# A two-layer graph attention kernel: VectorE's order woven, softmax totals behind the attends, and a new end

## The chip, the cores and the metric

The kernel runs on one core of a Trainium2 chip. The metric is device time in microseconds (us), the median of several runs. Its engines have short names in the profile: PE (TensorE, matmuls; PEld is its weight load), DVE (VectorE), ACT (ScalarE), POOL (GpSimd) and SP (SyncE, which here issues nearly all DMAs).

## The reference, cut to what matters

64 graphs of 256 nodes have 512 features each, and a dense 0/1 adjacency. Two layers follow one another, all in float32:

```python
# layer 0
feat_proj = feats @ fc_w.T + fc_b
logits = q + k.T                               # q, k: one column each, from feat_proj
masked = logits + (1.0 - adj) * -1e9
atten = softmax(where(masked >= 0, masked, 0.01 * masked))
x1 = atten @ feat_proj + feats
# layer 1, 8 heads of 64
Q, K, V = x1 @ W_q + b_q, x1 @ W_k + b_k, x1 @ W_v + b_v
scores = Q @ K.T / 8 + a[:, None] + c[None, :] + b_g + log(adj + 1e-9)   # a, c = x1 @ halves of w_g
out = softmax(scores) @ V + x1
```

## The kernel before

The 64 graphs make 32 groups of two (512 tokens). The kernel is one software pipeline: a step of it works at the same time on up to four groups, named D (done but for its last division and store), A (layer 1's attention), F (layer 0's weighted sum and all projections) and X (the next group: its loads and layer 0's weights). There is no scheduler: `step` and `attention_and_layer_0` write the order out by hand as strings of pieces, such as `A("both:0 parts:0 turn_residual:1")`. Each piece issues instructions to several engines, and every engine runs what it has been given in exactly that order. So a piece's place in the strings sets its place in each engine's queue, and in SP's queue of DMAs too.

The projections are products of 512 x 512 matrices by Strassen's scheme with seven block products, here called `p1` to `p7` (class `Product`, matmuls in L404). For each of `pf` (layer 0's features), `pq`, `pk` and `pv`: VectorE first makes four sums of the moving blocks (`ysum:0..3` for pf, `xsum:0..3` for the others, L344 and L369); the products accumulate in PSUM; ScalarE copies what is kept (`keep`), and VectorE adds the quarters (`sum_00`, `sum_11`, `sum_10`, L432; for pf L490, with GpSimd adding x to the kept part in L484). `p4` accumulates on the bank that `sum_11` has to read first.

x1 must also be had transposed. Each quarter of x1 is turned in 32 x 32 blocks by VectorE (`send`, L781), written to DRAM (xd, L785) and read back in four pieces (`fetch`, L793) into `x1T`. `keys:t` (L508, jc) are dot products of x1's rows with half of w_g. `dot_q:t` and `dot_k:t` are those of the next group's x with the rows of layer 0 (L508, jq and jk), and `spread` sends the q dots through DRAM to all partitions (qrow).

Layer 1's attention: `scores:u` (L850, exponentials in L859) for four units u (graph and half of the heads), `factor:u:jc` multiplies the exponentials by the adjacency (L867). The softmax denominators go by `both:u` (adds two tiles, es, L875) and `parts:u` (turns the sum in blocks, est, L905, then reduces it, L906); `totals:gr` sums over partitions by a matmul with a matrix of ones (L915), and `ratios:gr` takes reciprocals (L927). `attend:gr` is the product with V (L888, copied to oTs in L895). Then `turn:gr` (osb, L967), `divide:gr` (L987), `complete:gr` (adds the residual xb, L995), `store:gr` (L1028). `residual:gr` and `turn_residual:gr` make xb out of x1T (xv, L818 and L832). For layer 0, `add_tiles`, `parts_0` and `recip` do what both, parts and totals do.

Most tiles that matter have one buffer per tag: `x`, `adj`, `oTs`, `es`, `e0`, `osb`. A load into x waits until the last reader of the older x is done, and so for adj.

The last step (no next group) has an order of its own. Behind it a check that all reciprocals were in range (`in_range`) sets a flag, and a branch on the flag skips a general version of the kernel.

## Time and profile before

| | |
|---|---|
| median of 3 runs | 2330.38 us (2330.05 to 2332.13) |
| the profiled execution | 2331.22 us |
| its span, first to last instruction | 2329.4 us |
| granted TensorE clock, mean | 0.998 |
| PE, DVE, ACT, POOL busy | 2293.2, 2202.7, 1080.2, 125.5 us |
| DMA | 163.84 MB |

Busy is the time in which an engine had an instruction under way. Matmuls overlap each other in the records: a matmul of 256 columns is shown with some 380 ns, and the next starts 216 ns after it. So of PE a length of a stretch says more than a sum of durations.

### The profile page before, as it was taken

To read this page: it belongs to the slowest core of one execution; us is meant where nothing else is said; L and a number is where in the kernel's file an instruction comes from. 1 tells how busy PE (TensorE), PEld (TensorE's weight loads), DVE (VectorE), ACT (ScalarE), POOL (GpSimd) and SP (SyncE) were. 2 spreads that over 40 slices of the span, in tenths; PEclk is the share of its full clock that TensorE was granted. 3 is DMA by queue.
4 is the path that set the end of the run, shared out by engine and by line. 5 is a ranking of instruction groups with operands and counts; after the bars stand their busy time and mean duration, and the time that the engine had idled before them with its cause. 6 is when DMAs were issued, how large, how long until landed. Compare 5 with 4: busy or idle time off the path is not lost.

```text
span 2329.4 us, 33749 instructions
## 1 busy us (share of the span) xinstructions
PE 2293.2 (98%) x12554; PEld 1902.1 (82%) x12554; DVE 2202.7 (95%) x3212; ACT 1080.2 (46%) x2121; POOL 125.5 (5%) x120
## 2 busy tenths in 40 slices
PE   9999999999999999999999999999999999999996
PEld 5888888888888888888887888888888888888885
DVE  6799999999999999999999999999999999999996
ACT  3554345453445544455534455444554344554443
POOL 0000000000000000000000000000000000000000
PEclk9999999999999999999999999999999999999999
DMA  4123323222322232232233222332222333223312
GB/s 131 41 64 73 78 73 69 59 69 77 87 73 57 64 75 77 73 68 60 69 81 82 73 51 60 85 78 73 63 63 70 78 80 75 56 61 84 78 46 38
DMA packets 517265, 163.84 MB, mean 70 GB/s; under 512 B 415188, under 2 KB 478696, under 8 KB 517096
## 3 DMA queue, kind: packets, MB, share of 16 engines
q1 hardware_dynamic: 514440, 160.32, 29.0%
q8 instruction: 101, 1.65, 0.3%
q10 hardware_dynamic: 2656, 1.31, 0.2%
q14 instruction: 68, 0.56, 0.1%
HBM read 95.43 MB, written 66.12 MB: 69 GB/s over the span
## 4 chain that ended last, share of the span: by engine, by line
PE 56%; DVE 31%; DMA 5%; issue 4%; SPq 2%; ACT 1%; DVEq 0%; POOL 0%; ACTq 0%; POOLq 0%
PE pk L404 11%; PE pq L404 10%; PE pf L404 9%; PE pv L404 9%; PE y L678 6%; PE sc L850 5%; DVE e L867 5%; PE oT L888 5%; DVE est L905 2%; DVE es L875 2%; DVE x L490 2%; DMA xd<-xt 2%; DVE jc L508 2%; DVE tb L344 2%; DVE e L593 1%
## 5 line engine op out<-in xcount | busy, mean ns | idle before, releaser
L859 ACT ACTIVATE e<-sc,c 128x512 f32<-128x512 f32 x512 | 299.6, 736 | 68.6 <-PE sc L850 68.6
L867 DVE TENSOR_TENSOR e<-e,am 128x1024 f32<-128x1024 f32 x256 | 293.4, 1219 | 0.0
L484 POOL TENSOR_TENSOR pf_s<-pf_s,x 128x512 f32<-128x512 f32 x93 | 121.9, 1311 | 2118.2 <-ACT pf_s L483 2049.5
L850 PE MATMUL sc<-qT,kT 64*128 64x256 f32 x2048 | 230.7, 380 | 0.0
L678 PE MATMUL y<-e,x 128*128 128x256 f32 x992 | 228.8, 384 | 0.0
L888 PE MATMUL oT<-e,v 128*64 128x256 f32 x2048 | 228.3, 381 | 0.0
L850 PEld LDWEIGHTS sc<-qT,kT 64*128 64x128 f32 x2048 | 196.4, 187 | 32.1 <-issue 10.6
L678 PEld LDWEIGHTS y<-e,x 128*128 128x128 f32 x992 | 183.6, 190 | 32.7 <-ACT e L859 10.3
L888 PEld LDWEIGHTS oT<-e,v 128*64 128x64 f32 x2048 | 144.2, 137 | 80.2 <-issue 11.0
L895 ACT COPY oTs<-oT 128x512 f32<-128x512 f32 x128 | 72.0, 588 | 260.9 <-DVE osb L967 132.3
L421 ACT ACTIVATE pq_s<-pq,cols 128x256 f32<-128x256 f32 x192 | 80.6, 471 | 233.9 <-DVE qT L432 141.5
L905 DVE STREAM_TRANSPOSE est<-es 128x1024 f32<-128x1024 f32 x124 | 153.1, 1235 | 3.2
L906 DVE TENSOR_REDUCE part<-est 128x32 f32<-128x1024 f32 x124 | 151.3, 1220 | 4.2
L875 DVE TENSOR_TENSOR es<-e,e 128x1024 f32<-128x1024 f32 x126 | 153.3, 1217 | 0.4
L483 ACT ACTIVATE pf_s<-pf,recip 128x256 f32<-128x256 f32 x186 | 77.5, 467 | 156.4 <-PE pf L404 156.4
L418 ACT COPY pk_s<-pk 128x512 f32<-128x512 f32 x96 | 56.3, 586 | 170.0 <-PE pk L404 137.2
L404 PE MATMUL pq<-x1T,wq 128*128 128x256 f32 x512 | 122.8, 383 | 4.5 <-DMA x1T<-xd 3.9
L404 PE MATMUL pv<-wv,t1b_c 128*128 128x256 f32 x512 | 122.7, 382 | 0.0
L404 PE MATMUL pk<-t1b,wk 128*128 128x256 f32 x512 | 121.1, 379 | 0.5 <-DVE kT L432 0.5
L404 PE MATMUL pq<-t1b,wq 128*128 128x256 f32 x512 | 121.4, 380 | 0.0
L404 PE MATMUL pv<-wv,t1b 128*128 128x256 f32 x512 | 121.1, 379 | 0.0
L404 PE MATMUL pk<-t1b,k_s 128*128 128x256 f32 x512 | 120.9, 379 | 0.0
(175 smaller groups left out, 4514.5 us busy)
## 6 DMA issues: line engine op xcount, KB each, us to landing
x<-in_x_dram SPq DMA_DIRECT2D x32, 1024.0 KB, 5.3
xd<-xt SPq DMA_DIRECT2D x124, 256.0 KB, 2.0
x1T<-xd SPq DMA_DIRECT2D x496, 64.0 KB, 2.0
out_dram<-xb SPq DMA_DIRECT2D x248, 128.0 KB, 3.1
adj<-in_adj_dram SPq DMA_DIRECT2D x128, 128.0 KB, 3.6
qrow<-q SPq DMA_DIRECT2D x31, 256.0 KB, 4.1
fc_nat<-in_L_gnn_fc_w_dram ACTq DMA_DIRECT2D x4, 256.0 KB, 4.8
wq<-in_L_gnn_W_q_dram SPq DMA_DIRECT2D x1, 1024.0 KB
```

What stands on the lines that cost most here:

```text
L404: nc.tensor.matmul(o, lhsT=lk[:, ts(m, P)] if len(lk.shape) == 2 else lk[:, m], rhs=rk, start=(start and m == 0 and k == 0), stop=(m == 1 ...
L421: nc.scalar.activation(dst[:, m], src[:, m], AF.Identity, bias=self.bias[:, 2 * o + m : 2 * o + m + 1],)
L483: nc.scalar.mul(s[:, m], src[:, m], self.recip[:, TPG * k + m : TPG * k + m + 1])
L484: nc.gpsimd.tensor_tensor(s, s, self.out(o, k), ALU.add)
L678: nc.tensor.matmul(y[:, ts(gr, N)], lhsT=self.x[:, gr * TPG + j, ts(c, P)], rhs=self.e0[:, j, gr, :], start=(gr == 0 and j == 0), stop=(gr ...
L850: nc.tensor.matmul(sc[par][:, pr, :], lhsT=self.kT[rows, 2 * hg + pr, ts(t, P)], rhs=self.qT[rows, 2 * hg + pr, ts(gr, N)], start=True, st ...
L859: nc.scalar.activation(e[:, par], sc[par], AF.Exp, bias=self.c[:, t : t + 1], scale=SCALE)
L867: nc.vector.tensor_tensor(ef, ef, self.am[:, jc, u // 2, :].unsqueeze(1).to_broadcast([P, 4, N]), ALU.mult,)
L875: nc.vector.tensor_tensor(self.esum[u], self.e[u, 0], self.e[u, 1], ALU.add)
L888: nc.tensor.matmul(oT[par * HD : (par + 1) * HD, pr, :], lhsT=self.v[:, gr * TPG + jc, ts(h, HD)], rhs=self.e[2 * gr + hg, jc][:, par, pr, :],
L905: nc.vector.transpose(turned, self.esum[u].rearrange("p a b i -> p (a b i)"))
L906: nc.vector.tensor_reduce(self.part[:, hg, :], turned.rearrange("p (m c) -> p m c", c=B), AX.X, ALU.add,)
```

## The change

The weights of layer 0 are cut into two pieces (`logits`, `leaky`), `parts` into `est` and `part_of`, `parts_0` into `turn_0` and `part_0`, and the pieces of one chain are placed apart, with pieces of other chains in between. `both`, `est` and `part_of` of the first two units go ahead of `attend:0`; `totals:0` becomes `totals_0`, behind the attends, with two matmuls of half the width, and `ratios_0` takes one reciprocal. `residual:1` writes its xv into the buffer of adj instead of that of oTs, and `turn_residual:1` goes behind the attends. `load_adj` goes from the top of a step to a place just ahead of `load_x`. The range check is made every 3 groups instead of every 4 or so (six slots of reciprocals instead of four). In the last step, the scores come in another order and ahead of most of pv, both graphs' sums are matmuls over the exponentials (`sums_of_e`), `finish` is cut in halves, and the check runs ahead of the last attend.

```diff
-    NR = 4
+    NR, NCHECK = 6, 3
...
                 def residual(self, gr):
-                    self.xv = one.tile([P, NC, N], F32, tag="oTs", name=f"xv_{self.g}_{gr}")
+                    tag = ("oTs", "adj")[gr]
+                    self.xv = one.tile([P, NC, N], F32, tag=tag, name=f"xv_{self.g}_{gr}")
...
+                def totals_0(self):
+                    half = NC * N // B // 2
+                    self.tot = bank(f"tot_{self.g}_0")[:, 0 : 2 * half]
+                    for par in range(2):
+                        nc.tensor.matmul(
+                            self.tot[par * HD : (par + 1) * HD, :].rearrange("p (a m) -> p a m", a=2),
+                            lhsT=every[:, 0:HD], rhs=self.part[:, :, par * half : (par + 1) * half],
+                            start=True, stop=True, skip_group_check=True,
+                        )
+
+                def ratios_0(self):
+                    self.rs = recip1[:, (self.g + 1) % NR, 0]
+                    nc.vector.reciprocal(self.rs.rearrange("p m b -> p (m b)"), self.tot)
...
             def attention_and_layer_0(D, A, F, X):
                 A("scores:0 scores:1 scores:2 scores:3")
-                F("add_tiles parts_0")
-                A("factor:0:0 factor:0:1 factor:1:0 factor:1:1")
-                A("factor:2:0 factor:2:1 factor:3:0 factor:3:1")
+                F("add_tiles")
+                A("factor:0:0")
+                F("turn_0")
+                A("factor:0:1")
+                F("part_0")
+                A("factor:1:0 factor:1:1 factor:2:0 factor:2:1 factor:3:0 factor:3:1")
                 F("mix:0 mix:1 recip mix:2 mix:3 ysum:0")
-                D("ratios:1 divide:1")
-                A("residual:1")
-                F("ysum:1")
+                D("ratios:1")
+                D("divide:1")
+                A("both:0 residual:1")
+                F("ysum:1 ysum:2")
+                A("est:0 part_of:0")
                 D("complete:1 store:1")
-                F("ysum:2 pf.p1 pf.keep_1 pf.p2 pf.p6 pf.sum_00 begin send:0:0 fetch:0:0 ysum:3")
-                A("both:0 parts:0 turn_residual:1")
-                F("pf.p7 pf.p5 pf.p3 pf.add_01 pf.sum_11 send:1:1")
-                A("attend:0")
-                F("pf.sum_01 send:0:1 fetch:1:1 fetch:0:1")
-                A("both:1 turn:0 attend:1 parts:1")
-                F("copy:0 pf.p4 pf.sum_10 send:1:0 fetch:1:0")
-                F("pq.p1 pq.keep_1 pk.p1")
-                A("totals:0")
-                F("pk.keep_1 pv.p1 pv.keep_1")
+                F("pf.p1 pf.keep_1 pf.p2 pf.p6 pf.sum_00 begin send:0:0 fetch:0:0 ysum:3")
+                A("both:1 est:1")
+                F("pf.p7 pf.p5 pf.p3 pf.add_01 pf.sum_11")
+                A("part_of:1")
+                F("pf.sum_01 send:1:1 send:0:1 fetch:1:1 fetch:0:1")
+                A("attend:0 turn:0 attend:1 totals_0 turn_residual:1")
+                F("copy:0 keys:2 pf.p4 pf.sum_10 keys:3 send:1:0 fetch:1:0")
+                F("pq.p1 pq.keep_1 pk.p1 pk.keep_1 pv.p1 pv.keep_1")
...
-                X("load_adj")
...
-                F("xsum:0 xsum:1 xsum:2 pq.p6")
-                F("keys:2 keys:3 keys:0 keys:1")
-                X("load_x")
-                A("ratios:0 both:2 parts:2")
+                F("xsum:0 keys:0 xsum:1 keys:1")
+                X("load_adj load_x")
+                F("xsum:2 pq.p6")
+                A("both:2 ratios_0 est:2 divide:0 part_of:2")
                 F("pq.p7 pq.p2 pq.sum_00 xsum:3")
-                check()
+                X("dot_q:0")
+                A("complete:0 store:0")
+                X("dot_q:1")
                 F("pq.p5 pk.p6 pq.sum_11 pq.p3")
-                A("divide:0")
-                X("dot_q:0 dot_q:1 dot_q:2 dot_q:3 spread")
+                X("dot_q:2")
+                A("turn:1")
+                X("dot_q:3 spread")
                 F("pq.p4 pq.sum_10 copy:1 copy:2")
-                A("complete:0 store:0 turn:1")
+                X("adjt dot_k:0")
+                A("both:3")
+                X("dot_k:1")
+                F("pk.p7 pk.p5 pk.sum_11 residual:0")
+                X("dot_k:2")
+                F("pk.p2 pk.sum_00")
+                X("dot_k:3")
+                F("turn_residual:0")
+                A("est:3")
+                F("pk.p3 pk.p4 pk.sum_10")
                 if n is None:
-                    A("both:3 parts:3")
-                F("pk.p7 pk.p5 pk.sum_11 residual:0")
-                X("adjt")
-                F("pk.p2 pk.sum_00")
-                X("dot_k:0 dot_k:1")
-                F("pk.p3 pk.p4 pk.sum_10")
-                X("dot_k:2 dot_k:3")
-                F("turn_residual:0")
-                if n is None:
-                    A("totals:1 ratios:1 divide:1 complete:1 store:1")
-                    F("residual:1 turn_residual:1")
-                    F("pv.p2 pv.p6 pv.sum_00 scores:0 scores:1 scores:2 scores:3")
-                    F("pv.p7 factor:0:0 factor:0:1 factor:1:0 factor:1:1 both:0 both:1")
-                    F("pv.p5 pv.sum_11 pv.p3 sums_1:0 pv.p4 pv.sum_10")
-                    F("factor:2:0 factor:2:1 ratios_t:0 ratios_r:0 factor:3:0 factor:3:1")
-                    F("attend:0 finish:0 sums_of_e:1 attend:1")
-                    F("ratios_t:1 ratios_r:1 finish:1")
-                    check_ranges()()
+                    A("part_of:3 totals:1 ratios:1")
+                    F("residual:1 pv.p6 scores:2 scores:3 scores:0 scores:1")
+                    A("divide:1 complete:1 store:1")
+                    F("factor:2:0 factor:2:1 factor:3:0 factor:3:1 pv.p7 pv.p5 pv.p3")
+                    F("factor:0:0 factor:0:1 pv.sum_11 turn_residual:1 factor:1:0 factor:1:1")
+                    F("sums_of_e:1 sums_of_e:0 attend:1 ratios_t:1 ratios_r:1 ratios_t:0 ratios_r:0")
+                    F("pv.p2")
+                    flag_ready = check_ranges()
+                    F("finish:1:0 pv.sum_00 pv.p4 finish:1:1 pv.sum_10 attend:0")
+                    flag_ready()
+                    F("finish:0:0 finish:0:1")
                     return
                 X("mask add_eps")
                 F("pv.p6 pv.p7")
-                X("weights:0")
-                F("pv.p5 pv.p2")
-                X("weights:1")
-                F("pv.sum_11 pv.p3 pv.p4 pv.sum_00")
-                A("both:3 parts:3")
+                X("logits:0:0 logits:0:1")
+                A("part_of:3")
+                X("logits:1:0 leaky:0 logits:1:1")
+                F("pv.p5 pv.p2 pv.sum_11")
+                X("leaky:1")
+                F("pv.p3 pv.p4 pv.sum_00")
+                check()
                 F("pv.sum_10")
```

More of the change, by code (lines that the diff above doesn't have):

```diff
@@ L226, in rows_of_chunks @@
                 return t
-            rows_0 = rows_of_chunks([q_w[0], k_w[0], fc_b], "rows_0", "sms")
+            rows_0 = rows_of_chunks([q_w[0], k_w[0], fc_b], "rows_0", "oTs")
             x_0 = load_x(0)
-            rows_1 = rows_of_chunks([b_q, b_v], "rows_1", "sms1")
+            rows_1 = rows_of_chunks([b_q, b_v], "rows_1", "es")
             qb = row(q_b, "qb")
@@ L587, in weights, with logits, leaky @@
                 def weights(self, jc):
-                    e = self.e0[:, jc].rearrange("p g i -> p (g i)")
-                    for gr in range(GP):
-                        t = gr * TPG + jc
-                        eg = self.e0[:, jc, gr].rearrange("p (t n) -> p t n", t=TPG)
-                        nc.vector.scalar_tensor_tensor(
-                            eg, self.qrow[:, :, ts(gr, TPG)].rearrange("p n t -> p t n"),
-                            self.kq[:, 0, t : t + 1], eg, ALU.add, ALU.add,
-                        )
+                    for gr in range(GP):
+                        self.logits(jc, gr)
+                    self.leaky(jc)
+                def logits(self, jc, gr):
+                    t = gr * TPG + jc
+                    eg = self.e0[:, jc, gr].rearrange("p (t n) -> p t n", t=TPG)
+                    nc.vector.scalar_tensor_tensor(
+                        eg, self.qrow[:, :, ts(gr, TPG)].rearrange("p n t -> p t n"),
+                        self.kq[:, 0, t : t + 1], eg, ALU.add, ALU.add,
+                    )
+                def leaky(self, jc):
+                    e = self.e0[:, jc].rearrange("p g i -> p (g i)")
                     nc.vector.scalar_tensor_tensor(e, e, 0.01, e, ALU.mult, ALU.max)
@@ L604, in add_tiles, with turn_0 @@
                     nc.vector.tensor_tensor(es0, e0[:, 0], e0[:, 1], ALU.add)
-                def parts_0(self):
-                    turned = two.tile([P, TOK], F32, tag="xt", name=f"es0t_{self.g}")
+                def turn_0(self):
+                    self.es0t = two.tile([P, TOK], F32, tag="xt", name=f"es0t_{self.g}")
                     if self.older is None:
@@ L615, in parts_0, with part_0 @@
                         self.parts_all = self.older.part_all
-                    nc.vector.transpose(turned, self.es0)
+                    nc.vector.transpose(self.es0t, self.es0)
+                def part_0(self):
                     nc.vector.tensor_reduce(
-                        self.parts_all[:, ALL - TOK // B : ALL], turned.rearrange("p (m c) -> p m c", c=B), AX.X, ALU.add
+                        self.parts_all[:, ALL - TOK // B : ALL],
+                        self.es0t.rearrange("p (m c) -> p m c", c=B), AX.X, ALU.add,
                     )
@@ L650, in sums @@
                             )
-                    self.sms = one.tile([P, P], F32, tag="sms", name=f"sms_{self.g}")
+                    self.sms = one.tile([P, P], F32, tag="oTs", name=f"sms_{self.g}")
                     nc.scalar.copy(self.sms, sm)
@@ L765, in begin @@
                     self.d = {}
+                    self.e, self.esum, self.oTs, self.sms1, self.osb = {}, {}, {}, {}, {}
                     self.x1T = one.tile([P, 2, GP, TPG * HALF], F32, tag="x1T", name=f"x1T_{g}")
@@ L838, in scores @@
                     g, (gr, hg) = self.g, divmod(u, 2)
-                    if u == 0:
-                        self.e, self.esum, self.oTs, self.sms1, self.osb = {}, {}, {}, {}, {}
                     for jc in range(TPG):
@@ L872, in both @@
                 def both(self, u):
-                    tag = "adj" if self.g == NG - 1 and u == 1 else "es"
-                    self.esum[u] = one.tile([P, 2, 2, N], F32, tag=tag, name=f"es_{self.g}_{u}")
+                    self.esum[u] = one.tile([P, 2, 2, N], F32, tag="es", name=f"es_{self.g}_{u}")
                     nc.vector.tensor_tensor(self.esum[u], self.e[u, 0], self.e[u, 1], ALU.add)
@@ L879, in attend @@
                     g = self.g
-                    self.oTs[gr] = one.tile([P, 2, 512], F32, tag="oTs", name=f"oTs_{g}_{gr}")
+                    tag = "adj" if g == NG - 1 and gr == 0 else "oTs"
+                    self.oTs[gr] = one.tile([P, 2, 512], F32, tag=tag, name=f"oTs_{g}_{gr}")
                     for hg in range(2):
@@ L895, in attend, with est @@
                         nc.scalar.copy(self.oTs[gr][:, hg, :], po)
-                def parts(self, u):
+                def est(self, u):
                     g, (gr, hg), nb = self.g, divmod(u, 2), NC * N // B
@@ L903, in parts, with part_of @@
                     tag = "adj" if u == 3 else "e0"
-                    turned = one.tile([P, NC * N], F32, tag=tag, name=f"est_{g}_{u}")
-                    nc.vector.transpose(turned, self.esum[u].rearrange("p a b i -> p (a b i)"))
+                    self.turned = one.tile([P, NC * N], F32, tag=tag, name=f"est_{g}_{u}")
+                    nc.vector.transpose(self.turned, self.esum[u].rearrange("p a b i -> p (a b i)"))
+                def part_of(self, u):
                     nc.vector.tensor_reduce(
-                        self.part[:, hg, :], turned.rearrange("p (m c) -> p m c", c=B),
+                        self.part[:, u % 2, :], self.turned.rearrange("p (m c) -> p m c", c=B),
                         AX.X, ALU.add,
                     )
+                def totals_0(self):
[6 more added lines that the diff above has]
+                            start=True, stop=True, skip_group_check=True,
+                        )
+                def ratios_0(self):
+                    self.rs = recip1[:, (self.g + 1) % NR, 0]
+                    nc.vector.reciprocal(self.rs.rearrange("p m b -> p (m b)"), self.tot)
                 def totals(self, gr):
@@ L920, in ratios @@
                 def ratios(self, gr):
-                    self.rs = recip1[:, self.g % NR, gr]
+                    self.rs = recip1[:, (self.g + 1) % NR, gr]
                     sums = self.all_sums.rearrange("p (a b m) -> p b a m", a=2, b=2)
@@ L929, in ratios @@
                         )
-                def sums_1(self, gr):
-                    g = self.g
-                    sm = bank(f"sm_{g}_{gr}")[:, 0:N]
-                    for hg in range(2):
-                        for n in range(4):
-                            nc.tensor.matmul(
-                                sm[ts(n, RS), :], lhsT=ones[:, hg, :],
-                                rhs=self.esum[2 * gr + hg][:, n // 2, n % 2, :],
-                                start=(hg == 0), stop=(hg == 1), tile_position=(0, n * RS),
-                                skip_group_check=True,
-                            )
-                    self.sms1[gr] = two.tile([P, N], F32, tag="xt", name=f"sms1_{g}_{gr}")
-                    nc.scalar.copy(self.sms1[gr], sm)
                 def sums_of_e(self, gr):
@@ L972, in ratios_r @@
                     nc.vector.reciprocal(rc, self.st.rearrange("p (b c) -> p c b", c=B)[:, 0:2, :])
-                    rs = recip1[:, g % NR, gr].rearrange("p (h n) b -> p h n b", h=2)
+                    rs = recip1[:, (g + 1) % NR, gr].rearrange("p (h n) b -> p h n b", h=2)
                     nc.vector.tensor_copy(rs, rc.unsqueeze(2).to_broadcast([P, 2, 2, nb]))
@@ L980, in ratios_r @@
                         )
-                    self.rs = recip1[:, g % NR, gr]
+                    self.rs = recip1[:, (g + 1) % NR, gr]
                 def divide(self, gr):
@@ L998, in ratios_t, with finish @@
                 def ratios_t(self, gr):
-                    self.st = one.tile([P, N], F32, tag="sms1", name=f"st_{self.g}_{gr}")
+                    self.st = one.tile([P, N], F32, tag="es", name=f"st_{self.g}_{gr}")
                     nc.vector.transpose(self.st, self.sms1[gr])
-                def finish(self, gr):
+                def finish(self, gr, hg):
                     g, nb = self.g, N // B
-                    self.osb[gr] = one.tile(
-                        [P, NC * N], F32, tag=("osb", "e0")[gr], name=f"osb_{g}_{gr}"
-                    )
-                    for hg in range(2):
-                        o = self.osb[gr][:, ts(hg, 512)]
-                        blocks = o.rearrange("p (m c) -> p m c", c=B)
-                        nc.vector.transpose(o, self.oTs[gr][:, hg, :])
-                        nc.vector.tensor_tensor(
-                            blocks, blocks,
-                            self.rs[:, ts(hg, 2)].rearrange("p n b -> p (n b)").unsqueeze(2).to_broadcast(
-                                [P, 2 * nb, B]
-                            ), ALU.mult,
-                        )
-                        nc.vector.tensor_tensor(o, o, self.xb[gr][:, ts(hg, 512)], ALU.add)
-                    self.store(gr, 2 * (nc.sync, nc.scalar) if gr else 4 * (nc.sync,))
+                    if hg == 0:
+                        self.osb[gr] = one.tile(
+                            [P, NC * N], F32, tag=("e0", "osb")[gr], name=f"osb_{g}_{gr}"
+                        )
+                    o = self.osb[gr][:, ts(hg, 512)]
+                    rs = recip1[:, (g + 1) % NR, gr, ts(hg, 2)].rearrange("p n b -> p (n b)")
+                    blocks = o.rearrange("p (m c) -> p m c", c=B)
+                    nc.vector.transpose(o, self.oTs[gr][:, hg, :])
+                    nc.vector.tensor_tensor(
+                        blocks, blocks, rs.unsqueeze(2).to_broadcast([P, 2 * nb, B]), ALU.mult
+                    )
+                    nc.vector.tensor_tensor(o, o, self.xb[gr][:, ts(hg, 512)], ALU.add)
+                    if hg == 1:
+                        self.store(gr, (4 * (nc.sync,), 2 * (nc.sync, nc.scalar))[gr == 0])
                 def store(self, gr, queues=4 * (nc.sync,)):
@@ L1034, in in_range @@
                 for src, a, b in ((recip0[:, lo:hi].rearrange("p g t -> p (g t)"), 0, n0),
-                                  (recip1[:, lo % NR : lo % NR + hi - lo].rearrange(
+                                  (recip1[:, (lo + 1) % NR : (lo + 1) % NR + hi - lo].rearrange(
                                       "p g a h b -> p (g a h b)"), n0, n0 + n1)):
@@ L1049, in attention_and_layer_0 @@
                 A("scores:0 scores:1 scores:2 scores:3")
-                F("add_tiles parts_0")
-                A("factor:0:0 factor:0:1 factor:1:0 factor:1:1")
-                A("factor:2:0 factor:2:1 factor:3:0 factor:3:1")
-                F("mix:0 mix:1 recip mix:2 mix:3 ysum:0")
-                D("ratios:1 divide:1")
-                A("residual:1")
-                F("ysum:1")
-                D("complete:1 store:1")
-                F("ysum:2 pf.p1 pf.keep_1 pf.p2 pf.p6 pf.sum_00 begin send:0:0 fetch:0:0 ysum:3")
-                A("both:0 parts:0 turn_residual:1")
-                F("pf.p7 pf.p5 pf.p3 pf.add_01 pf.sum_11 send:1:1")
-                A("attend:0")
-                F("pf.sum_01 send:0:1 fetch:1:1 fetch:0:1")
-                A("both:1 turn:0 attend:1 parts:1")
-                F("copy:0 pf.p4 pf.sum_10 send:1:0 fetch:1:0")
-                F("pq.p1 pq.keep_1 pk.p1")
-                A("totals:0")
-                F("pk.keep_1 pv.p1 pv.keep_1")
+                F("add_tiles")
[4 more added lines that the diff above has]
+                A("factor:1:0 factor:1:1 factor:2:0 factor:2:1 factor:3:0 factor:3:1")
+                F("mix:0 mix:1 recip mix:2 mix:3 ysum:0")
+                D("ratios:1")
[3 more added lines that the diff above has]
+                A("est:0 part_of:0")
+                D("complete:1 store:1")
+                F("pf.p1 pf.keep_1 pf.p2 pf.p6 pf.sum_00 begin send:0:0 fetch:0:0 ysum:3")
[6 more added lines that the diff above has]
+                F("pq.p1 pq.keep_1 pk.p1 pk.keep_1 pv.p1 pv.keep_1")
             def check_ranges():
-                in_range(NG - NR // 2, NG, "last")
+                in_range(NG - NCHECK, NG, "last")
                 pk = bank("pok")
@@ L1106, in step @@
                     f.features_first()
-                    F("pq.p1 pq.keep_1 copy:0 pk.p1 pk.keep_1 pv.p1 pv.keep_1")
-                F("xsum:0 xsum:1 xsum:2 pq.p6")
-                F("keys:2 keys:3 keys:0 keys:1")
-                X("load_x")
-                A("ratios:0 both:2 parts:2")
+                    F("pq.p1 pq.keep_1 copy:0 pk.p1 pk.keep_1 pv.p1 pv.keep_1 keys:2 keys:3")
+                F("xsum:0 keys:0 xsum:1 keys:1")
+                X("load_adj load_x")
+                F("xsum:2 pq.p6")
@@ L1163, in check @@
                     def check():
-                        if d is not None and (d.g % NR == NR - 1 or d.g == NG - NR // 2 - 1):
-                            in_range(d.g // NR * NR, d.g + 1, f"{d.g}")
+                        if d is not None and d.g % NCHECK == 1:
+                            in_range(max(d.g + 1 - NCHECK, 0), d.g + 1, f"{d.g}")
                     step(d, a, f, n, check)
```

## The prediction

> **What bounds the kernel now.** I read the page's busy shares first, then busy time cut into stretches, then the chain of waits, then the timelines of one step.

> ```profile
> span 2329.4 us, 33749 instructions
> PE 2293.2 (98%) x12554; PEld 1902.1 (82%) x12554; DVE 2202.7 (95%) x3212; ACT 1080.2 (46%) x2121; POOL 125.5 (5%) x120
> ```

> Two engines are nearly full, PE (98%) and DVE (95%), so which one waits must be looked up. Stretches from one group's first score matmul to another's (length, then busy PE, PEld, DVE, ACT, POOL):

> ```profile
> 79.55:2218.82 2139.27, 2126.45 (x11641) 1778.69 (x11640) 2061.90 (x2976) 1007.72 (x1980) 118.02 (x90) 1.00 0.30 70
> ...
> 1076.52:1147.35 70.83, 70.82 (x390) 59.31 (x389) 68.57 (x99) 33.58 (x66) 3.87 (x3) 1.00 0.31 71
> ...
> 1218.18:1291.63 73.45, 71.34 (x389) 59.13 (x388) 69.89 (x105) 33.59 (x66) 3.91 (x3) 1.00 0.29 69
> ...
> 2285.39:2329.45 44.06, 26.90 (x210) 17.92 (x209) 28.61 (x50) 14.22 (x26) 0.00 (x0) 0.89 0.24 38
> ```

> The first row holds 30 steps: 2139.27 / 30 = 71.31 us each. The second is a dense one: PE never idle, 70.83 us, which is PE's floor. A few steps are longer (third row). So all that better VectorE order can win in the 30 steps is 30 x (71.31 - 70.83) = 14.4 us. The last stretch, the end, is 44 us with 27 us of PE.

> The chain of waits in the dense step stays on PE. Two of its points matter below: pq.p1 starts at 1110.48 (that is where pf.p4 ends) and its tot matmuls take 0.17 us.

> ```profile
> 1108.56 1.92 PE pf L404 x8
> 1110.48 1.73 PE pq L404 x8
> ...
> 1113.93 0.17 PE tot L915 x2
> ```

> SyncE's queue in that step, with issue times:

> ```profile
> 1078.25 2.87 SPq L195 DMA_DIRECT2D adj<-in_adj_dram  x4
> ...
> 1113.90 0.34 SPq L785 DMA_DIRECT2D xd<-xt  x1
> 1115.91 1.73 SPq L793 DMA_DIRECT2D x1T<-xd  x4
> 1118.73 0.40 SPq L200 DMA_DIRECT2D x<-in_x_dram  x1
> ```

> The adjacency is issued 40 us before the features x, far from everything. Issue to landing is 5.3 us (median) for x. VectorE's first reader of x, dot_q:0, and the PE product pq.p4:

> ```profile
> 1126.42 0.69 DVE L508 CUSTOM_DVE_ANT_0 jq<-x,wq_row 128x512 f32<-128x512 f32 x1
> ...
> 1126.53 1.89 PE L404 MATMUL pq<-t1b,wq 128*128 128x256 f32 x8
> ```

> x is read 7.7 us after its issue, 2.4 us more than its 5.3. In before the sum that pq.p4 waits for (sum_11) stands ahead of all dots.

> **The change part by part.**

> *Weaving, POOL.* Two tensor_tensors of a step meet a GpSimd add (start, length; in brackets the idle time before):

> ```profile
> 1094.18 1.75 DVE L344 TENSOR_TENSOR tb<-yT 128x512 f32<-128x512 f32 x1
> ...
> 1097.51 1.57 DVE L344 TENSOR_TENSOR tb<-yT,tb 128x512 f32<-128x512 f32 x1
> ...
> 1094.05 1.33 POOL L484 TENSOR_TENSOR pf_s<-pf_s,x 128x512 f32<-128x512 f32 x1 [62.80 <-ACT pf_s L483]
> ```

> The group's median is 0.68, so 1.07 + 0.89 = 2.0 us of DVE per step is lost. In the new order a transpose (est) and a reduction stand there; a transpose that met POOL at 1100.78 took its usual 1.25. Dependent neighbours: es to est start 1.25 us apart, two independent instructions of that size 1.14 (divide at 1125.29, next at 1126.42). Some eight pairs are parted: 0.9 us per step. [...]

> *ratios_0* is one reciprocal in place of two (row: 354 ns each): 0.35 us of DVE, same cap.

> *totals_0*: two matmuls (4 records, loads of 64 columns) for one (2 records, 128 columns). Loads of 64 columns take 137 ns in the oT row, of 128 columns 190: 4 x 137 - 2 x 190 = +0.17 us of PE per step; bounds 0 and +0.4. It moves ahead of pf.p4, so 0.22 us (0.17 and 0.05 of its successor's) leave the stretch behind pf.p4.

> *residual:1 into the adj buffer.* ACT and DVE waits on oTs go; they are not on PE's path. But adj is now busy until turn_residual:1 has read it, so load_adj stands behind fetch:1:0, directly ahead of load_x, on SP's queue. dot_q:0, complete:0 and dot_q:1 now stand ahead of sum_11 on VectorE. This is the step that decides. From the end of pf.p4 (P, 1110.48 in before), with before's durations:

> - pf.sum_10 0.04 + 0.75, keys:3 0.73, send 0.71, to SP's issue 0.03: P+2.26. Before, VectorE came here only at 1112.26; by my sum of the new order it waits for pf.p4 with about 0.8 us to spare.
> - xd issue to first fetch issue 2.01, four fetches 1.73, step 0.05: P+6.05.
> - four adj issues 2.87 + 0.05: P+8.97, x is issued (keys:1, its other condition, ends near P+5.8).
> - landing 5.3: P+14.27, if x runs alone. The adj transfers hold the DMA engines from 1.25 to 4.75 us after their first issue (96% share in 1079.5 to 1083.0); x begins 0.77 after its own issue, here 3.69 after adj's. So x is held 1.06 more: P+15.33. Bounds 0 and 1.9 (the xd at 1097.62, right behind stores, reached its fetch in 3.93 instead of 2.01); 1.06 rests on adj's own packets.
> - dot_q:0 0.72, complete:0 1.14, dot_q:1 0.73, sum_11 0.69, semaphores 0.1: pq.p4 may start at P+18.7.

> PE has 1126.53 - 1110.48 - 0.22 = 15.83 us of work in between. It waits 18.7 - 15.83 = 2.9 us, in each of the 30 steps that load a next group. [...]

> All of PE's later work is queued behind pq.p4. VectorE has 19 us of work from there to the next scores, PE 20.8, so no second stall. store:0 moves ahead of q and qrow on SP: its issues (2.9 us from L+1.9, L being x's landing) end before dot_q:3 does (L+5.8), and qrow (1.4 + 4.25 more) lands about 4 us before logits ask.

> *The part sums ahead of the features.* divide:1 (1.14) and es:0 (1.14) now stand ahead of ysum:1, which pf.p6 waits for (its first matmul at 1094.31). But the factors start 2.4 us after the scores (1078.95, when the first exponentials are there) instead of at 1080.80, and only es0's transpose and reduction (1.2) stand among them: they end at 1089.3 instead of 1089.9. From there tb 0.6, ratios 0.75, divide 1.14, es 1.14, tb 0.7: 1093.7, 0.6 before pf.p6 asks. Nothing, with little to spare.

> *keys:0 between xsum:0 and xsum:1* delays pq.p6 by 0 to 0.7 us, but inside the same 18.7 us: nothing, except in the first step, which has no such chain: +0.7.

> New step: 70.83 + 0.17 + 2.9 = 73.9. Over before's mean: 30 x (73.9 - 71.31) = +78. Its odd long steps (late stores, late xd) fall into PE's wait now or lengthen the x chain: another +2 (four fetches in 30 steps were 0.7 late).

> *The end.* pv.p2 goes behind the scores (1.73 us of PE), finish is cut in halves, the range check runs ahead of the last attend. From the scores the last add came after 34.8 us (2285.39 to 2320.21). New: exponentials to 10.5; s4, sum_11, turn_residual:1 and two factors on VectorE to 16.7; sums to 17.9, attend:1, pv.p2, pv.p4 and attend:0 to 29; copy and last half to 32.1. That is 2.7 + 1.7 = 4.4 earlier. Behind the last add lie 9.24 us, in which check, flag and the flag's branch (4.84 us on PE) follow one another; of these only the store (5.7) and the closing stay, about 1.5 less. Together -6 (bounds -2 and -9).

> Sum: 78 + 2 + 0.7 - 6 = +75. The profiled execution took 2331.2 us, 1.8 more than its span and 0.8 over the median of the runs, 2330.4. So 2331.2 + 75 - 0.8 = 2405.

> **Rivals.**

> *x is in time* (the other side). If x lands by P+12.4, pq.p4 starts on time; that is 2.9 us earlier than I add up, about what adj's four issues cost (2.87). Then the odd steps' 14.4 us go, totals_0 costs 5, the end gives 6: 2330.4 - 14.4 + 5 + 0.7 - 6 = 2316. For it: dot_q had 2.4 us to spare. Against: SP's order, and x is now read three instructions ahead of sum_11. 0.13. Exactly balanced: 0.02.

> *x is not held by adj's transfers*: landing at P+14.27 or a little before (5.0 was the least); the wait is 1.8, the step 72.8, 1.5 over the mean: 2330.4 + 30 x 1.5 - 3 = 2372. 0.22.

> *VectorE comes late to pf.sum_10*: complete:1 and es:1 read two SBUF tiles and may meet GpSimd adds (1.3 us each, 0.8 spare); 0.5 more per step, 15 us: 2420. 0.13.

> **How the numbers follow.** My forecast has 0.50 (2385 to 2415), and 2405 is its time. The range reaches down through the undelayed rival to 2350 and up to 2425, past most of the late one; what is left out is mainly the faster case. About 0.2% (4.7 us) is what a measurement of this kernel can tell from no change. Faster 0.13, within 0.02, slower 0.85.

> **What would show it.** Right: in the waits, PE pq L404 waiting for VectorE some 2.5 to 3 us thirty times, VectorE's jq waiting for x's DMA as often; steps of 73 to 74 us; x issued right behind adj; tb rows back at 0.68; the end shorter by 4 to 8 us. Wrong: steps at 71.0 with no idle PE, or a PE wait at another product.

## The result, and the profile after

The changed kernel takes 2426.27 us (median of 4 runs, 2418.99 to 2427.68); the kernel before, run beside it, 2330.9. The ratio is 1.040, with a 95% interval of 1.038 to 1.042: 4% slower. The side and the mechanism are as forecast; 2426 is 21 us above the forecast of 2405 and 1 us above the end of its range.

The head of the page after, with the line of shares of its chain of waits:

```profile
span 2425.9 us, 34038 instructions
...
PE 2310.3 (95%) x12632; PEld 1930.1 (80%) x12632; DVE 2072.9 (85%) x3191; ACT 1077.1 (44%) x2121; POOL 144.0 (6%) x120
...
PE 49%; DVE 20%; DMA 15%; SPq 11%; issue 3%; ACT 1%; POOL 0%; ACTq 0%; DVEq 0%
```

VectorE got what the change was made for: 2072.9 us busy, 130 less than before. The span nevertheless grew by 96.5 us, and the chain that ended last now runs over VectorE (20%), DMAs (15%) and SyncE's issuing (11%).

Busy time by stretch: the 30 steps, two single steps, and the end, which is all that follows the 30 steps (length, then PE, PEld, DVE, ACT and POOL busy, granted clock, DMA share, GB/s):

```profile
79.42:2320.89 2241.47, 2144.74 (x11702) 1805.27 (x11701) 1940.93 (x2965) 1004.50 (x1980) 135.88 (x90) 0.99 0.29 67
1650.90:1727.10 76.20, 72.32 (x392) 60.76 (x391) 64.46 (x97) 33.46 (x66) 4.56 (x3) 0.98 0.29 66
1727.10:1800.87 73.77, 70.63 (x392) 59.57 (x391) 64.20 (x97) 33.47 (x66) 4.56 (x3) 1.00 0.29 68
2320.89:2425.90 105.01, 90.22 (x586) 72.51 (x585) 81.78 (x122) 43.52 (x87) 4.56 (x3) 0.96 0.23 47
```

A step is 2241.47 / 30 = 74.72 us, against 71.31 before: 102.2 us over the 30 steps. The end is 105.0 us where it was 110.6, 5.6 less (4.4 of them behind the last group's scores, 39.63 us for 44.06); the start is 0.1 less. 102.2 - 5.6 - 0.1 = 96.5. So the loss is one of the repeated step. In the third row PE is busy 70.63 of 73.77 us at full clock: it waits 3.1. The second row is a step in which, besides, the clock fell.

The waits (who waits, for whom, total, number of waits, longest):

```profile
DVE jq L508 <- DMA x<-in_x_dram: 74.9, 30, 4.0
DVE t1b L369 <- DMA x1T<-xd: 67.6, 30, 3.5
...
PE pq L404 <- DVE qT L432: 59.8, 30, 3.4
...
PE pq L404 <- DVE t1b L369: 38.1, 30, 2.5
```

The row `PE pq <- DVE qT` is `pq.p4` waiting for `sum_11`, thirty times, 1.99 us each; `DVE jq <- DMA x` above it is `dot_q:0` waiting for the features, as often, 2.5 us each. That is the wait that was forecast. The last row is a second one: `pq.p6` waits for `xsum`, 1.27 us each. It had been priced at nothing.

One step on SyncE's queue (`pf.p4` ended at P = 1310.53; issue time, duration, number):

```profile
1309.27 3.89 SPq L804 DMA_DIRECT2D x1T<-xd  x8
1313.26 0.39 SPq L796 DMA_DIRECT2D xd<-xt  x1
1315.40 1.73 SPq L804 DMA_DIRECT2D x1T<-xd  x4
1317.17 3.39 SPq L195 DMA_DIRECT2D adj<-in_adj_dram  x4
1320.72 0.54 SPq L200 DMA_DIRECT2D x<-in_x_dram  x1
```

on VectorE (in brackets the idle time before the instruction, and what ended it):

```profile
1314.82 0.69 DVE L369 TENSOR_TENSOR t1b<-x1T 128x512 f32<-128x512 f32 x1 [2.14 <-DMA x1T<-xd]
...
1326.17 0.69 DVE L508 CUSTOM_DVE_ANT_0 jq<-x,wq_row 128x512 f32<-128x512 f32 x1 [2.30 <-DMA x<-in_x_dram]
...
1326.79 1.22 DVE L1007 TENSOR_TENSOR xb<-osb,xb 128x1024 f32<-128x1024 f32 x1
1327.93 0.68 DVE L508 CUSTOM_DVE_ANT_0 jq<-x,wq_row 128x512 f32<-128x512 f32 x1
1328.54 0.69 DVE L432 TENSOR_TENSOR qT<-pq,pq_s 128x512 f32<-128x512 f32 x1
```

and on PE, `pq.p3` and behind it `pq.p4`:

```profile
1325.58 1.89 PE L404 MATMUL pq<-x1T,q_s 128*128 128x256 f32 x8
1329.28 2.00 PE L404 MATMUL pq<-t1b,wq 128*128 128x256 f32 x8 [1.81 <-DVE qT L432]
```

Read it from SyncE down: eight fetches, the last xd, its four fetches, then 3.39 us in which four adjacency loads are issued, then x, directly behind. VectorE stands idle for 2.30 us ahead of x's first reader, and the sum that PE needs (`qT<-pq,pq_s`) is the fourth of the instructions from there. PE stands idle for 1.81 us until that sum is done.

One small thing came as forecast, and one stands beside it, in the groups of instructions (busy, mean ns of one, idle before):

```profile
L344 DVE TENSOR_TENSOR tb<-yT 128x512 f32<-128x512 f32 x62 | 41.7, 673 | 0.0
L344 DVE TENSOR_TENSOR tb<-yT,tb 128x512 f32<-128x512 f32 x62 | 41.4, 668 | 0.5 <-ACT yT L694 0.5
...
L484 POOL TENSOR_TENSOR pf_s<-pf_s,x 128x512 f32<-128x512 f32 x93 | 140.4, 1510 | 2202.0 <-ACT pf_s L483 2148.9
```

The `tb` sums are back at 0.67 us. GpSimd's adds take 1510 ns instead of 1311, which was not forecast; no other engine waits for them.

### The profile page after: what moved, and what is told of

The parts are those of the page before. It is cut to its first block, busy times and chain, and to the rows that moved or that the text cites. A ratio compares the mean times of both kernels' runs of the same rounds, so it can differ in the third digit from the quotient of the medians.

```text
span 2425.9 us, 34038 instructions
## 1 busy us (share of the span) xinstructions
PE 2310.3 (95%) x12632; PEld 1930.1 (80%) x12632; DVE 2072.9 (85%) x3191; ACT 1077.1 (44%) x2121; POOL 144.0 (6%) x120
## 4 chain that ended last, share of the span: by engine, by line
PE 49%; DVE 20%; DMA 15%; SPq 11%; issue 3%; ACT 1%; POOL 0%; ACTq 0%; DVEq 0%
PE pv L404 14%; PE pk L404 12%; DMA x<-in_x_dram 8%; DMA xd<-xt 7%; SPq L804 7%; PE pf L404 7%; DVE e L877 6%; PE sc L860 5%; PE y L688 4%; PE pq L404 4%; SPq L195 3%; PE oT L898 3%; DVE xb L1007 2%; DVE jq L508 2%; DVE es L884 1%
## 5 line engine op out<-in xcount | busy, mean ns | idle before, releaser
L484 POOL TENSOR_TENSOR pf_s<-pf_s,x 128x512 f32<-128x512 f32 x93 | 140.4, 1510 | 2202.0 <-ACT pf_s L483 2148.9
L404 PE MATMUL pq<-t1b,wq 128*128 128x256 f32 x512 | 138.0, 417 | 59.8 <-DVE qT L432 59.8
L404 PEld LDWEIGHTS pq<-t1b,wq 128*128 128x128 f32 x512 | 102.1, 204 | 85.9 <-DVE qT L432 71.8
L404 PE MATMUL pq<-t1b,q_s 128*128 128x256 f32 x512 | 119.7, 388 | 38.1 <-DVE t1b L369 38.1
L915 DVE STREAM_TRANSPOSE est<-es 128x1024 f32<-128x1024 f32 x124 | 151.1, 1218 | 1.1
L508 DVE CUSTOM_DVE_ANT_0 jq<-x,wq_row 128x512 f32<-128x512 f32 x128 | 86.8, 678 | 75.1 <-DMA x<-in_x_dram 74.9
L404 PEld LDWEIGHTS pq<-t1b,q_s 128*128 128x128 f32 x512 | 96.2, 193 | 61.2 <-issue 49.3
L483 ACT ACTIVATE pf_s<-pf,recip 128x256 f32<-128x256 f32 x186 | 77.4, 467 | 151.5 <-PE pf L404 151.5
L432 DVE TENSOR_TENSOR v<-pv,pv_s 128x512 f32<-128x512 f32 x96 | 66.2, 689 | 87.9 <-PE pv L404 65.0
```

The costliest lines, as they stand in the source:

```text
L404: nc.tensor.matmul(o, lhsT=lk[:, ts(m, P)] if len(lk.shape) == 2 else lk[:, m], rhs=rk, start=(start and m == 0 and k == 0), stop=(m == 1 ...
L484: nc.gpsimd.tensor_tensor(s, s, self.out(o, k), ALU.add)
L508: nc.vector.tensor_tensor_reduce(out=junk, in0=src, in1=w_row, scale=1.0, scalar=init, op0=ALU.mult, op1=ALU.add, accum_out=dst,)
L915: nc.vector.transpose(self.turned, self.esum[u].rearrange("p a b i -> p (a b i)"))
```

## The experiments

All times are medians beside the kernel before on the same chip (2332.8 us for e1 to e4, 2334.1 for e5 to e8); the ratio is to that kernel. Between runs of the two groups, ratios are compared.

### What makes x late: adj ahead of it, or the dots ahead of sum_11?

Experiment e1 puts the load of x ahead of that of adj, and leaves the rest:

```diff
-                X("load_adj load_x")
+                X("load_x load_adj")
```

> The changed kernel with load_x ahead of load_adj, nothing else. Theory A (pq.p4 waits because x is issued 2.9 us late behind adj's four issues and moved behind adj's packets, while it is read ahead of sum_11): x is issued at about P+7 (P is the end of pf.p4), lands near P+12.3, about when VectorE asks for it; the wait at pq.p4 goes from 2.0 us a step to 0 to 0.3, the one at pq.p6 (1.3 us) stays, steps of about 72.0 us, total 79 + 30 x 72.0 + 105 = about 2345. Theory B (sum_11 is late because two dots and complete stand ahead of it on VectorE, whenever x lands): the wait at pq.p4 stays near 2 us, total above 2410. Slow-clock stretches should nearly vanish under A.

Measured: 2337.7 us, ratio 1.0024 (1.0015 to 1.0033). The 96 us of the change are gone but for 6. Over the 30 steps x is issued at P+7.1 (P+9.8 in the changed kernel), lands at P+12.6 (P+15.8), and `pq.p4` no longer waits. Waits of e1:

```profile
DVE t1b L369 <- DMA x1T<-xd: 69.3, 30, 3.4
...
PE pq L404 <- DVE t1b L369: 39.8, 30, 2.4
```

The rows of x and of `PE pq <- DVE qT` are gone from the list's head. What remains is `pq.p6` with 1.3 us: as long as the x chain set the time of `pq.p4`, it had cost little; now it is the step's own loss (71.66 us a step).

Experiment e2 leaves the loads as the change has them, and moves the readers of x behind the sum:

```diff
-                X("dot_q:0")
-                A("complete:0 store:0")
-                X("dot_q:1")
+                A("complete:0 store:0")
                 F("pq.p5 pk.p6 pq.sum_11 pq.p3")
-                X("dot_q:2")
+                X("dot_q:0 dot_q:1 dot_q:2")
```

> The changed kernel with dot_q:0 and dot_q:1 behind sum_11 on VectorE (complete:0 stays ahead), loads as in the change (adj, then x). A and B both: no wait at pq.p4 any more, since sum_11 no longer waits for x; VectorE waits up to 1 us for x at dot_q:0, off PE's path; the wait at pq.p6 stays 1.3 us; about 2345. If it stays above 2400, x has nothing to do with it.

Measured: 2350.25 us, ratio 1.0062 (1.0041 to 1.0084). Waits of e2:

```profile
PE pq L404 <- DVE t1b L369: 38.6, 30, 2.2
...
DVE jq L508 <- DMA x<-in_x_dram: 25.9, 26, 3.2
```

x still lands at P+16.2, and VectorE still waits 26 us for it, but now behind the sum: PE's wait at `pq.p4` is gone. What is left over e1, some 12 us, is in part in the same list: waits of `pv` for ScalarE's `pv_s` (5.5 us, eleven times; 0.7 in e1) and of `pk` for `kT` (2.7), behind the four instructions that now bunch up there. The mean granted clock of e2 is 0.996, of e1 0.998. So either half of the change alone, the later x or the earlier readers, costs little; the two together cost some 90 us, slow clock included (below). Which of them is "the cause" has no answer: x late by 3 us and `sum_11` queued behind it are both needed.

### The second wait

`xsum:0` starts when the last of the eight fetches has landed (in the changed kernel 0.04 us behind it, in the steps where the trace has the landing), for the quarter that it needs is fetched second. Experiment e3 is e1 with the fetch that `xsum:0` needs put first; e4 adds e2's order:

```diff
-                F("pf.sum_01 send:1:1 send:0:1 fetch:1:1 fetch:0:1")
+                F("pf.sum_01 send:1:1 send:0:1 fetch:0:1 fetch:1:1")
```

> load_x ahead of load_adj, and fetch:0:1 issued ahead of fetch:1:1 (xsum:0 needs the first alone). Theory A': the wait at pq.p6 is the last of eight fetch pieces landing, then xsum:0, keys:0 and xsum:1 in a row; with the order turned xsum:0 and keys:0 run while fetch:1:1 is still coming, and pq.p6 waits 0.3 us or less: steps of 71.0 to 71.3, total 2315 to 2324. Rival: pq.p6 waits because VectorE is late with its own work; then nothing moves beside e1 (about 2345).

> All three edits: load_x first, fetch:0:1 first, dot_q:0 and dot_q:1 behind sum_11. Theory A: neither wait is left, steps of 70.7 to 71.0 us as PE's floor, total 79 + 30 x 70.9 + 105 = about 2311, faster than the kernel before (2331) by about 20. If the weaving has a cost of its own on PE, it stays above 2325.

Measured: e3 2321.15 us, ratio 0.9955 (0.9939 to 0.997); e4 2316.18 us, ratio 0.9929 (0.9913 to 0.9946). From e1 to e3 the time fell by 16.6 us, and the wait of `pq.p6` from 39.8 us to the 17.0 of this row of e3:

```profile
PE pq L404 <- DVE t1b L369: 17.0, 24, 1.6
```

22.8 us of wait brought 16.6 us of time, because part of it came back: `pq.p2` waits four times for a fetch (3.2 us), and `pq.p3` and `pq.p4` lose some 2 us in short stops, with `dot_q` now waiting 0.24 us a step for x. e4, which takes `dot_q` off the path, is faster than before by 0.7%, as much as a rival of the prediction had said (2316). But the order of the fetches that e3 and e4 mend is that of the kernel before too, and no run gives it to the kernel before; so what the change gains by itself, without the two orders that went wrong, is not shown.

Experiment e6 asks whether `keys:0`, between `xsum:0` and `xsum:1`, is on the path (e1's loads, the keys behind):

```diff
-                F("xsum:0 keys:0 xsum:1 keys:1")
+                F("xsum:0 xsum:1 keys:0 keys:1")
```

> load_x first, and keys:0 behind xsum:1 (xsum:0 xsum:1 keys:0 keys:1); compare with load_x first alone (2337.7, wait at pq.p6 1.28 us). If keys:0 between them is on the path: the wait falls by 0.7 to about 0.55 us and the total by 20 to about 2317. If xsum:1 waits for its own DMA: nothing changes.

Measured: 2334.66 us, ratio 1.0006 (0.9997 to 1.0014), against e1's 1.0024: almost nothing. The wait did shrink:

```profile
PE pq L404 <- DVE t1b L369: 23.7, 28, 2.1
```

It is 16 us less than e1's 39.8, and the time fell by some 4 (1.0024 less 1.0006, of 2333 us). My expectation, that the 0.6 us would go in full, missed. From the start of one product to the start of the next, as means over the 30 steps, e6 reaches `pq.p6` 0.53 us earlier than e1, and then loses 0.21 at `pq.p7` and the product behind it, 0.11 at `pq.p4` and 0.10 at `pk.p7`. In e6 `xsum:1` stands right behind `xsum:0`, whose result it reads, and `keys:1` right behind `keys:0`; `xsum:2`, behind all four in both runs, starts 0.2 us later than in e1, and `pq.p7`, which needs it, starts 0.17 us after `xsum:2`'s end (0.75 in e1). These stops do not show as idle in the records, so they count as PE busy (70.77 us a step for 70.37).

### What the stretches of slow clock cost

In the changed kernel the granted clock was 0.5 for 54.6 us within the steps, in 14 stretches, all of them behind a wait of PE; before there was none within the steps. Experiment e5 keeps the change as it is, and fills PE's two waits with matmuls whose result nobody reads (of `wq` on `wq`), ahead of `pq.p6` and ahead of `pq.p4`:

```diff
+                    fill(2)
                 F("xsum:2 pq.p6")
...
+                    fill(4)
                 F("pq.p4 pq.sum_10 copy:1 copy:2")
```

> The changed kernel as it is, with matmuls that nobody reads put into PE's two waits: four ahead of pq.p4 and two ahead of pq.p6 in each of the 30 steps (1.7 and 0.9 us of PE, less than its mean waits of 2.0 and 1.2). Theory C: part of what the change costs (about 25 us) is not the waits but the slow clock after them (stretches of 3.4 us at 0.5 of the clock in the records, 1.7 us each); with PE kept busy the granted clock returns to 0.998 and the total falls to 2400 or a little below, though PE does more. Rival: slow matmuls come with the waits whatever PE does in them; then 2426 stays, or more.

Measured: 2410.39 us, ratio 1.0328 (1.0311 to 1.0345). With more work the kernel is 16 us faster than the change as it is (by the two ratios, 17). Its head, and its waits:

```profile
PE 2363.4 (98%) x12992; PEld 1979.7 (82%) x12992; DVE 2069.2 (86%) x3191; ACT 1078.1 (45%) x2121; POOL 143.9 (6%) x120
...
DVE jq L508 <- DMA x<-in_x_dram: 77.1, 30, 3.4
...
PE pq L404 <- DVE t1b L369: 17.7, 19, 2.2
...
PE pq L404 <- DVE qT L432: 11.0, 18, 1.2
```

x is as late as before (77.1 us of VectorE waiting), so the chain is untouched; the mean granted clock over the span is 0.997, against 0.987 in the changed kernel and 0.998 in the kernel before. The fill was not free: PE did 2.6 us more per step while its waits shrank by 2.3, some 8 us in all. So slow clock was worth 16 + 8 = 24 us by the medians, and 29 by the profiled executions, whose 30 steps fell by 21; half of 54.6 is 27. These are estimates from the runs' times and waits, and lie within 5 us of each other.

### Can the rest of the wait be taken away?

In e4 `pq.p6` still waits 0.54 us a step, behind the chain from the sends through xd to the fetches. e7 is e4 with the issues of `store:1`, which stand ahead of them on SyncE's queue, given to ScalarE's queue (`store_by_act` is `store` with ScalarE in SyncE's place):

```diff
-                D("complete:1 store:1")
+                D("complete:1")
...
-                F("pf.p7 pf.p5 pf.p3 pf.add_01 pf.sum_11")
+                F("pf.p7 pf.p5")
+                D("store_by_act:1")
+                F("pf.p3 pf.add_01 pf.sum_11")
```

e8 is e7 with the two sends ahead of `part_of:1` on VectorE:

```diff
+                F("send:1:1 pf.sum_01 send:0:1")
                 A("part_of:1")
-                F("pf.sum_01 send:1:1 send:0:1 fetch:0:1 fetch:1:1")
+                F("fetch:0:1 fetch:1:1")
```

> The three edits of the last run (2316.2), and store:1 issued from ScalarE's queue behind pf.p5's copy instead of SP's queue right ahead of xd of quarter 00. Theory S: what is left at pq.p6 (0.54 us a step) comes from SP: four stores' issues and packets ahead of xd make fetch 00, and all behind it on SP, late. Then the xd lands 2.0 after its issue, the fetches start some 0.6 earlier, the wait falls to 0.2 or less and the total to 2305. Rival: VectorE's own work (the sends end too late) sets it; then 2316 stays.

> As the run before, and send:1:1 and send:0:1 ahead of part_of:1 on VectorE (1.14 us earlier). With SP free the fetches start with the sends: no wait at pq.p6 left, steps of 70.4 to 70.5 us, total 79 + 30 x 70.45 + 104 = about 2297 to 2301. If SP is still the limit, it equals the run before.

Measured: e7 2317.63 us, ratio 0.9925 (0.9902 to 0.9948), the same as e4: a miss. The waits of e7 and e8 for the same sum:

```profile
PE pq L404 <- DVE t1b L369: 17.7, 20, 2.2
```

```profile
PE pq L404 <- DVE t1b L369: 4.5, 10, 0.8
```

In e7 the first xd was issued 1.5 us earlier, but that was not the last link: the sends ended at the same times as in e4 (29.93 and 30.52 us after the scores), and from the issue of the third xd, that of the second of these sends, to the first of the eight fetches it took 2.80 us instead of 2.40. The stores are now issued by ScalarE just ahead of it; whether their packets delay it is not shown. e8 moves that last link: the second of these sends, whose quarter is fetched first, ends at 29.65 us after the scores instead of 30.52, and the first of the eight fetches starts at 32.23 instead of 33.35. Whether e8 needs the stores on ScalarE's queue was not tried. e8 takes 2299.65 us, ratio 0.9851 (0.9834 to 0.9867): 1.5% faster than before, and the fastest of all. A stretch as long as its 30 steps (cut 2.1 us ahead of the first scores):

```profile
79.10:2193.50 2114.40, 2108.34 (x11702) 1786.59 (x11701) 1947.10 (x2962) 1004.06 (x1980) 135.85 (x90) 1.00 0.31 71
```

2114.40 / 30 = 70.48 us a step, clock 1.00, 0.2 us of them idle.

## Why the prediction was right, and what in it was not

**The deciding step held.** x behind adj, `dot_q:0` ahead of `sum_11`: both waits came thirty times, in the two rows named beforehand. By its links, as means over the 30 steps (the landing over the 19 for which the trace has it): xd issued at P+2.80 (forecast 2.26), first fetch at 4.98 (4.27), adj at 6.75 (6.05), x issued at 9.81 (8.97), landed at 15.81 (15.33), `pq.p4` at 19.05 (18.7). The links on SyncE's queue came 0.5 to 0.8 us later than summed, and the first of them shows why: VectorE's last `send` ended at P+2.15, a little ahead of the sum, but SyncE was busy until P+2.64 with issuing the eight fetches that stand ahead of this xd, and the sum had no term for them. So the rival of a late VectorE falls too. Landing and the instructions behind it took a little less than summed (6.0 and 3.24 for 6.36 and 3.37), so 0.35 was left. e1 and e2 show both halves of the step by taking away one each. The rival of an x not held by adj's packets falls: x took 6.0 us (median) from issue to landing behind adj, against 5.3 in the kernel before and 5.5 ahead of adj (e1). It was held, though by 0.5 to 0.7 and not by 1.06. (The 1.06 counts x as beginning 0.77 us after its issue; in the trace of before, in the step of the prediction, its first packets come 1.07 us after it, and the same sum would give 0.76.)

**VectorE's own gain is there and is worth nothing here.** In the 30 steps VectorE is busy (2061.90 - 1940.93) / 30 = 4.03 us less per step; 2.0 and 0.9 for weaving and 0.35 for the reciprocal were forecast, the time being capped by PE's floor. By tile, each instruction counted until it ends or the next one starts: the `tb` sums give 1.98 (forecast 2.0), the reciprocals 0.44, and the rest, 1.6, lies mainly in `es`, `est`, `part` and the like and in the reads of the dots' accumulators, 0.6 each. The changed kernel holds parted and unparted pairs side by side: behind an `es` sum the `est` that reads it starts after 1.25 us (median of 31), an instruction that does not read it after 1.14 (62); behind an `est` the `part` that reads it after 1.27 (31), others after 1.11 and 1.17 (31 each). So parting these pairs does save, 0.10 to 0.16 us a pair. In the changed kernel the gain stands as VectorE waiting for DMAs (74.9 us for x, 67.6 for `x1T`).

**The waits were 3.26, not 2.9.** PE's total is (59.8 + 38.1) / 30. The one at `pq.p4` was 1.99 and the one at `pq.p6` 1.27, since PE stops at both: what `pq.p6` loses makes `pq.p4`'s wait shorter. The prediction left `pq.p6` at nothing "inside the same 18.7 us", which is right as long as x is late. It failed for its own rival: with x in time it gave 2316, and e1 measured 2337.7, because there `pq.p6` becomes the step's loss. The 2316 came only with the other fetch order (e4, 2316.18).

**The term that was missing: the clock.** 24 to 29 us of the 102 in the steps come from half clock behind PE's waits (estimated from e5). The sum took PE's work at its full-clock length and had no such term, and this alone is more than the 21 us by which 2405 was short. The profile before gave a sign of it: at its end, in the stretch with PE busy for 26.90 of 44.06 us, the clock was 0.89.

**The floor was a little too high.** "PE never idle, 70.83" was taken as PE's floor. In the changed kernel's step at 1727.10 PE is busy 70.63 with `totals_0` in it, and the shortest step of e8 takes 70.12. From start to start of the products, before's dense step loses 0.05 to 0.17 us against that one at seven places (most at `pq.p6` and `pq.p7`), 0.72 us in all. None of it shows as idle, since the records of matmuls overlap (some 380 ns long, 216 from start to start). `totals_0` itself came to +0.02 us (from 167 to 187 ns per step), not +0.17. So the 14.4 us that I had called the most to be won in the steps are not the most: e8 wins 30 x (71.31 - 70.48) = 25.

**The sum again, with measured terms:** PE's work 70.63, waits 3.26, clock 26 / 30 = 0.87 (26 out of the 24 to 29): 74.76 against the measured 74.72. Forecast were 70.83 + 0.17, 2.9 and none: 73.9. The odd steps' +2 had no place in it: they are part of the waits. The end gave 5.6 (forecast 6), the start 0.1 (forecast a loss of 0.7).

## What to carry to other kernels

An engine with an order by hand is a queue: before a load is moved, count what is issued ahead of it (here 3.39 us of adjacency loads), and before a reader of a load is moved, count who stands behind it (here `sum_11`, and behind that PE, 1.99 us a step). Before's dense step never waits for anything in the profile, and still loses 0.05 to 0.17 us at seven of its products, so the shortest step seen was not yet a floor. The change made PE wait 3.26 us a step, and stretches of half clock behind the waits cost an estimated 24 to 29 us more in 30 steps: where PE is made to wait in each pass, look at the granted clock too, and try whether work that nobody needs, put into the wait, makes the kernel faster (e5: 16 us): it tells the two costs apart.

## What the runs showed of the hardware that was not expected

In the changed kernel the longest wait at `pq.p4` was followed by a stretch of half clock. The wait on PE's timeline (start, length; in brackets the idle time before):

```profile
1704.50 3.50 PE L404 MATMUL pq<-t1b,wq 128*128 128x256 f32 x8 [3.38 <-DVE qT L432]
1707.79 2.12 PE L404 MATMUL pk<-t1b,k_s 128*128 128x256 f32 x8
1709.74 1.89 PE L404 MATMUL pk<-t1b,wk 128*128 128x256 f32 x8
```

and its clock in the stretch (the column behind POOL's):

```profile
1704.80:1708.20 3.40, 3.40 (x9) 2.69 (x8) 2.16 (x6) 2.08 (x5) 0.00 (x0) 0.50 0.93 141
```
